# Layer 3 of a four-layer network: patch loads on GpSimd, a quarter's last turn finished ahead of the next matrices, nine of 24 matrix copies on ScalarE

## The chip, the cores and the metric

The kernel runs on one core of one Trainium2 chip. Its metric is the device time of one execution in microseconds (us). Beside the runs there is one profiled execution with its trace, and every stage and duration below is from that one.

## The reference, cut to what matters

A 16 x 64 x 64 x 256 tensor passes four layers, each `x = x + layer(groupnorm(x))`. The change lies in layer 3, an involution with a 7 x 7 window: every pixel makes its own 49 weights for each of 16 groups of 16 channels.

```python
r = relu((x @ w_reduce - mean) * (gamma / sqrt(var + eps)) + beta)     # 64 channels
kgen = (r @ w_span + b_span).reshape(B, H, W, 16, 49)                   # weights of each pixel
patches = 7 x 7 neighbours of x                                         # B, H, W, 49, 16, 16
out = einsum('bhwgk,bhwkgc->bhwgc', kgen, patches)
```

The layer's result is added to its input: that input is called the residual below.

## The kernel before, in words

The four layers run one after another, with some overlap; what each leaves for the next lies in HBM. Layer 2 is written in a hand-made order. Layer 3 is not: its instructions are put in order for each engine by a scheduler that works through the program's dependences, buffers and priorities, so a change of one buffer count or one queue moves other instructions too.

Layer 3 takes the image in tiles of 3 x 8 output pixels, whose inputs are 9 x 14 = 126 pixels: those fill the 126 rows of a TensorE operand. Layer 2 leaves in HBM, for each image i and each half h of the 256 channels, the array `strips`, out of which one tile row of eight tiles (`xw`, 128 rows of 4 KB, 512 KB) is loaded at once. There are 22 tile rows.

An image is worked in four quarters, (h, pr) = (0,0), (0,1), (1,0), (1,1): h is the half of the channels and pr which 64 channels of it. A quarter has two stages.

- `matrices(h, pr)`: for two pairs of groups, q = 0 and 1, twelve steps n each fill a PSUM tile `pk` (L1372, pool `wg`, three buffers) with four small products of the spread `span` of `w_span` and the reduced pixels `rt`, and a copy adds the bias `spanb` and puts it in the SBUF tile `wm`. The 24 copies of a quarter are split: where `n % 12 in (1, 3, 6, 8, 10)` ScalarE makes the copy in four instructions (L1382), else VectorE in one (L1387). `wm[q]` holds the banded weight matrices of all 176 tiles.
- eleven turns over `td`, each of two tile rows. `involution7` multiplies the patches by the matrices into PSUM `pa` (L1444; it uses the pool `wg` as well); ScalarE (L1453) and VectorE (L1454) mask and join the two groups' parts into `ex`. `finished` transposes `ex` into `po` (L1463), adds the residual that lies in `ot` (L1471) and returns the stores to the output. A turn is finished in the course of the next one, and its stores are issued (L1514) at the start of the one after.

Three things are fetched in the course of the turns, all by SyncE's queue, which issues in order and waits where an instruction waits:

- the residual of the next turn, `load_residual` (L1431), 96 KB in pieces of 256 bytes, into `ot` with three buffers. The output's store leaves from the same buffer, so a load has to wait for the store that empties it.
- in a quarter with pr = 1, after each turn, the two tile rows of the next half (L1420): the patches have 24 buffers for 22 tile rows, and both quarters of one half use the same ones.
- in the quarter (1,1) also a part of the next image's reduced pixels' input `c3` (L1320, 384 KB, two buffers), which `reduced` (L1339 `pr`, L1346) turns into `rt`. The next image's matrices need all of `rt`.

The loop of turns, whose order is the program's priority:

```python
for dst, src in store:
    nc.sync.dma_start(out=dst, in_=src)      # the stores of the turn before last
if td == 0:
    wm = matrices(h, pr)
ex = involution7(i, h, pr, td, wm, msk)
if pr == 1 and (i, h) != (NI - 1, 1):
    load_patches(...)
if last:
    store = finished(*last)                  # the turn before this one
if h == pr == 1 and i + 1 < NI:
    reduced(i + 1, td, cs.pop((i + 1, td)))
```

So the last turn of a quarter is finished after the next quarter's matrices and first turn were put into the program.

Of the kernel before, what the change touches and what calls it, by code (L numbers as in the profile page):

```python
# [9 lines left out]
F32 = mybir.dt.float32  # L10
# [5 lines left out]
P = 128  # L16
# [28 lines left out]
def network(ctx: ExitStack, tc: tile.TileContext, a: dict, out: bass.AP):  # L45
    nc = tc.nc
# [136 lines left out]
    with ExitStack() as st:  # L183
# [27 lines left out]
        wk = st.enter_context(tc.tile_pool(name="a_work", bufs=2))  # L211
# [428 lines left out]
    with ExitStack() as st:  # L640
        pc = st.enter_context(tc.tile_pool(name="s_const", bufs=1))
        wk = st.enter_context(tc.tile_pool(name="s_work", bufs=3))
# [22 lines left out]
        with tc.tile_pool(name="s_conv", bufs=1) as pcv:  # L665
# [4 lines left out]
                out=lsa.rearrange("p i j c -> p (i j c)"), in_=a["lsa_w"].partition_broadcast(P)  # L670
# [3 lines left out]
            for dj in range(7):  # L674
                dst = band if dj == 0 else term
# [52 lines left out]
        with tc.manual_schedule():  # L728
# [25 lines left out]
            for n, (ch, g) in enumerate(steps):  # L754
# [18 lines left out]
                b, k = g * 8, min(8, NI - g * 8)  # L773
# [8 lines left out]
        n = NI * NCH  # L782
# [100 lines left out]
    with ExitStack() as st:  # L883
        pc = st.enter_context(tc.tile_pool(name="b_const", bufs=1))
        wk = st.enter_context(tc.tile_pool(name="b_work", bufs=2))
# [403 lines left out]
    with ExitStack() as st:  # L1289
        pc = st.enter_context(tc.tile_pool(name="c_const", bufs=1))  # L1290
        wk = st.enter_context(tc.tile_pool(name="c_work", bufs=2))
# [5 lines left out]
        def cconst(name, shape, src=None):  # L1297
            t = pc.tile(shape, F32, tag=name, name=name)
            if src is not None:
                nc.sync.dma_start(out=t, in_=src)  # L1300
            return t

        wr3 = cconst("wr3", [P, 2, 64], a["w_reduce"].rearrange("(h p) f -> p h f", p=P))
        wr3t = cconst("wr3t", [P, 2, 2, 64])
        for k in range(2):
            nc.vector.tensor_copy(wr3t[:, :, k, :], wr3)
        span = cconst("span", [P, 16, SPAN], a["span"].rearrange("k (g s) -> k g s", g=16))
        spanb = cconst("spanb", [P, 16 * TILE_OUT], a["spanb"])
        gpar = cconst("gpar", [P, 2], a["gpar"])
# [45 lines left out]
        def matrices(h, pr):  # L1355


            wm = []
            for q in range(2):
                w = wm_p.tile([P, NTL, 2 * TILE_OUT], F32, tag="wm", name="wm")  # L1360
                wm.append(w)
                first = h * 8 + pr * 4 + q * 2
                for n in range(12):

                    pk = wg.tile([P, 2, CT], F32, tag="wg", name="pk")
                    pkv = pk[:, :, 0 : 2 * NTL].rearrange("p b (m t) -> p b m t", m=2)
                    for m in range(2):
                        for b in range(2):
                            gg, o = divmod(n * 4 + b * 2 + m, TILE_OUT)
                            s0 = SPAN - P - (o // TC * (TC + 6) + o % TC)  # L1370
                            half = slice(b * 64, b * 64 + 64)
                            nc.tensor.matmul(  # L1372
                                pkv[:, b, m],
                                lhsT=span[half, first + gg, s0 : s0 + P],
                                rhs=rto[half, o, :],
                                start=True, stop=True,
                            )
                    g0 = first * TILE_OUT + n * 4
                    dst = w[:, :, n * 4 : n * 4 + 4].rearrange("p t (b m) -> p b m t", b=2)
                    if n % 12 in (1, 3, 6, 8, 10):  # L1380
                        for m in range(4):
                            nc.scalar.activation(  # L1382
                                dst[:, m // 2, m % 2], pkv[:, m // 2, m % 2], AF.Identity,
                                bias=spanb[:, g0 + m : g0 + m + 1],
                            )
                    else:
                        nc.vector.tensor_tensor(  # L1387
                            dst, pkv,
                            spanb[:, g0 : g0 + 4].rearrange("p (b m) -> p b m", b=2).unsqueeze(
                                3  # L1390
                            ).broadcast_to([P, 2, 2, NTL]),
                            ALU.add,
                        )
            return wm
# [4 lines left out]
        def blocks(t, td):  # L1399

            if td * TR * HW + 4 * TB <= NT:
                return [t[0:TB]]
            return [t[0:TB, 0:2], t[0 : HW, 2]]

        def tokens(t, i, h, pr, td):

            t = t[i, :, h * P + pr * 64 : h * P + pr * 64 + 64]
            t0 = td * TR * HW
            if t0 + 4 * TB <= NT:
                return [t[t0 : t0 + 4 * TB].rearrange("(m p) c -> p m c", p=TB)]  # L1410
            return [
                t[t0 : t0 + 2 * TB].rearrange("(m p) c -> p m c", p=TB),
                t[t0 + 2 * TB : t0 + 2 * TB + HW],
            ]

        def load_patches(i, h, td):

            for ti in range(td, td + 2):
                xw = xw_p.tile([P, NTC, P], F32, tag="xw", name="xw")
                nc.sync.dma_start(  # L1420
                    out=xw.rearrange("p t c -> p (t c)"),
                    in_=strips[i, h].rearrange("r w t c -> (r w) (t c)")[
                        ti * TR * (TC + 6) : ti * TR * (TC + 6) + P
                    ],
                )
                xws[i, h, ti] = xw

        def load_residual(i, h, pr, td):
            ot = wk.tile([P, 4, 64], F32, tag="ot", name="ot", bufs=3)
            for dst, src in zip(blocks(ot, td), tokens(x3_d, i, h, pr, td)):  # L1430
                nc.sync.dma_start(out=dst, in_=src)  # L1431
            return ot
# [26 lines left out]
        def finished(i, h, pr, td, ex, ot):  # L1459

            po = sm.tile([P, 2, P], F32, tag="sm", name="po")
            for b in range(2):
                nc.tensor.transpose(po[0:TB, b, :], ex[:, b * TB : (b + 1) * TB], ident)  # L1463
            pov = po.rearrange("p b (k c) -> p k b c", k=2)
            otv = ot.rearrange("p (k b) c -> p k b c", k=2)
            if len(blocks(ot, td)) == 1:
                sides = [(slice(0, TB), slice(0, 2), slice(0, 2))]
            else:
                sides = [(slice(0, TB), 0, slice(0, 2)), (slice(0, HW), 1, 0)]
            for p, k, b in sides:  # L1470
                nc.vector.tensor_tensor(otv[p, k, b], pov[p, k, b], otv[p, k, b], ALU.add)  # L1471
            return list(zip(tokens(outs, i, h, pr, td), blocks(ot, td)))
# [3 lines left out]

        turns = [
            (i, h, pr, td)  # L1480
            for i in range(NI) for h in range(2) for pr in range(2) for td in range(0, NTR, 2)
# [4 lines left out]
        for td in range(0, NTR, 2):  # L1486
            load_patches(0, 0, td)
        res = [load_residual(*turns[0])]
        cs, last, store = {}, None, []
        for n, (i, h, pr, td) in enumerate(turns):  # L1490
            if h == pr == td == 0:

                pm = sm.tile([P, CT], F32, tag="sm", name="pm")
                for k in range(2):
                    for j in range(2):
                        nc.tensor.matmul(
                            pm[64 * k : 64 * k + 64, 2 * j : 2 * j + 2],
                            lhsT=ident[:, 64 * j : 64 * j + 64], rhs=rs3[:, i, :],
                            start=True, stop=True,
                        )  # L1500
                msk = small.tile([P, 2, 2, 2], F32, tag="msk", name="msk")
                nc.vector.tensor_tensor(
                    msk.rearrange("p j k g -> p (j k) g"),
                    pm[:, 0:4].unsqueeze(2).broadcast_to([P, 4, 2]),
                    gpar.unsqueeze(1).broadcast_to([P, 4, 2]),
                    ALU.mult,
                )
            if n + 1 < len(turns):
                res.append(load_residual(*turns[n + 1]))
                i1, h1, pr1, td1 = turns[n + 1]  # L1510
                if h1 == pr1 == 1 and i1 + 1 < NI:
                    cs[i1 + 1, td1] = load_reduced(td1, i1 + 1)
            for dst, src in store:
                nc.sync.dma_start(out=dst, in_=src)  # L1514
            if td == 0:
                wm = matrices(h, pr)
            ex = involution7(i, h, pr, td, wm, msk)
            if pr == 1 and (i, h) != (NI - 1, 1):
                load_patches(*((i, 1) if h == 0 else (i + 1, 0)), td)
            if last:  # L1520
                store = finished(*last)
            if h == pr == 1 and i + 1 < NI:
                reduced(i + 1, td, cs.pop((i + 1, td)))
            last = (i, h, pr, td, ex, res.pop(0))
# [110 lines left out]
```

## Time and profile before

| | |
|---|---|
| median of 3 runs | 10375.88 us (10372.54 to 10379.64) |
| profiled execution, its own time | 10364.39 us |
| its span, first to last instruction | 10362.3 us |
| mean granted clock of TensorE in it | 0.898 of full speed |
| TensorE matmul, weight load | 8062.1 us (78%), 5739.4 us (55%) |
| VectorE, ScalarE, GpSimd | 6725.2 us (65%), 5273.7 us (51%), 2347.8 us (23%) |
| layer 3, first pk matmul to the end | 6870 to 10362 us |
| DMA queue of SyncE | 1743.32 MB, 55.1% of the engines' span |

Engines: PE is TensorE's matmuls, PEld its weight loads, DVE VectorE, ACT ScalarE, POOL GpSimd, SP SyncE; a q marks an engine's queue of instructions, here mostly DMA issues. A row of a group gives the line, the engine, the tiles it writes and reads, their shapes and the count; then the total busy time and the mean in ns; then the engine's idle time just before such instructions and who ended most of it. A row of a table of stages gives for each stretch of time its length, the busy time and number of instructions of each engine, TensorE's granted clock, the mean busy share of the 16 DMA engines and the rate in GB/s. A row of the waits says who waited for whom: total us, times, the longest. A row of the timeline gives start, length, engine, line and tiles; neighbouring instructions of one kind are merged, so a length can hold waits between them.

### The profile page before, as it was taken

What the parts mean: (1) busy time and instruction counts of PE and PEld (TensorE: products, weight loads), DVE (VectorE), ACT (ScalarE), POOL (GpSimd) and SP (SyncE); (2) the same over time, 40 slices, a digit from 0 to 9 for tenths busy, and PEclk for the clock granted to TensorE, in tenths of its full rate; (3) what the DMA queues carried; (4) which work ended last, traced back from release to release, by engine and by line L of the source; (5) the groups of instructions that cost most, each with busy time, mean ns of one, the idle gap of its engine ahead of it and who ended that gap; (6) DMA issues with size and microseconds to landing.
All of it is one profiled execution on the core that took longest, in us unless ns stands there. A gap on an engine that the chain in (4) does not pass through costs nothing.

```text
span 10362.3 us, 216910 instructions
## 1 busy us (share of the span) xinstructions
PE 8062.1 (78%) x86488; PEld 5739.4 (55%) x86488; DVE 6725.2 (65%) x11456; ACT 5273.7 (51%) x12544; POOL 2347.8 (23%) x1193
## 2 busy tenths in 40 slices
PE   8888898888988675777778777727777777777777
PEld 5666666666666432554555555525555555555555
DVE  5666666666666555999999999924544545445454
ACT  4555555555555446666666665514444434444344
POOL 0111111111111002677777776710000000000000
PEclk9999999999999777989888888868998988988889
DMA  7433444334442247577777777665555555565554
GB/s 244 139 130 124 143 146 134 131 127 138 146 133 100 90 139 252 178 224 229 226 226 228 229 228 215 172 173 170 173 171 178 148 178 162 167 183 148 176 164 142
DMA packets 1648725, 1762.94 MB, mean 170 GB/s; under 512 B 641249, under 2 KB 1343026, under 8 KB 1646562
## 3 DMA queue, kind: packets, MB, share of 16 engines
q1 hardware_dynamic: 1635722, 1743.32, 55.1%
q8 instruction: 684, 11.21, 0.4%
q10 hardware_dynamic: 11992, 5.74, 0.3%
q14 instruction: 327, 2.68, 0.1%
HBM read 1234.54 MB, written 536.87 MB: 171 GB/s over the span
## 4 chain that ended last, share of the span: by engine, by line
PE 32%; DVE 27%; DMA 13%; issue 11%; ACT 11%; POOL 4%; SPq 2%; ACTq 0%; DVEq 0%; POOLq 0%
DVE pd L1106 7%; PE pa L1444 6%; DVE wm L1387 6%; PE pk L1372 5%; PE pq L297 5%; PE py L453 4%; DVE x L1274 3%; DMA c_d<-c 2%; ACT sq L462 2%; ACT wm L1382 2%; PE po L1463 2%; DMA out<-ot 2%; PE pr L1339 2%; DMA strips<-xc 2%; DVE y L458 1%
## 5 line engine op out<-in xcount | busy, mean ns | idle before, releaser
L297 PE MATMUL pq<-wq,xn 128*128 128x384 f32 x4096 | 1481.4, 501 | 61.3 <-DVE diag L346 20.9
L1372 PE MATMUL pk<-rt,span 64*128 64x176 f32 x12288 | 1260.7, 344 | 269.6 <-DVE wm L1387 150.2
L1106 DVE TENSOR_TENSOR pd<-xs,pw 128x576 f32<-128x576 f32 (+15 forms) x3072 | 1437.7, 545 | 8.7 <-PE pw L1060 5.2
L1387 DVE TENSOR_TENSOR wm<-pk,spanb 128x704 f32<-128x704 f32 x896 | 1155.9, 1342 | 352.9 <-PE pk L1372 280.9
L1372 PEld LDWEIGHTS pk<-rt,span 64*128 64x128 f32 x12288 | 1013.5, 200 | 502.9 <-DVE wm L1387 260.2
L1382 ACT ACTIVATE wm<-pk,spanb 128x176 f32<-128x176 f32 x2560 | 973.0, 543 | 575.7 <-PE pk L1372 494.9
L1117 POOL TENSOR_TENSOR pd<-pd 128x2048 f32<-128x2048 f32 (+2 forms) x384 | 1067.9, 2781 | 402.5 <-DVE pd L1106 382.4
L1444 PE MATMUL pa<-wm,xw 126*32 126x48 f32 x45056 | 764.1, 220 | 426.1 <-issue 359.8
L297 PEld LDWEIGHTS pq<-wq,xn 128*128 128x128 f32 x4096 | 754.6, 194 | 492.2 <-issue 46.3
L1454 DVE SCALAR_TENSOR_TENSOR ex<-pa,msk,ex 128x192 f32<-128x192 f32 x704 | 291.3, 414 | 1084.7 <-ACT ex L1453 1084.1
L1444 PEld LDWEIGHTS pa<-wm,xw 126*32 126x32 f32 x45056 | 633.7, 119 | 615.9 <-issue 498.4
L1453 ACT ACTIVATE ex<-pa,msk 128x192 f32<-128x192 f32 x704 | 296.4, 421 | 949.6 <-PE pa L1444 730.7
L1076 PE MATMUL pt<-ident,pad 128*128 128x128 f32 x4608 | 654.9, 298 | 148.2 <-ACT rt L1053 58.5
L1029 PE MATMUL px<-x2p,wis 128*128 128x512 f32 x1024 | 588.8, 725 | 197.5 <-ACT c L1131 165.7
L1076 PEld LDWEIGHTS pt<-ident,pad 128*128 128x128 f32 x4608 | 559.6, 154 | 304.7 <-ACT rt L1053 70.9
L1080 ACT COPY xs<-pt 128x512 f32<-128x512 f32 x1152 | 608.8, 587 | 189.3 <-PE pt L1076 188.7
L1274 DVE TENSOR_REDUCE x<-pd 128x512 f32<-128x4608 f32 x128 | 633.4, 4948 | 1.4
L453 PE MATMUL py<-wo,oT 128*128 128x256 f32 x2048 | 484.4, 388 | 55.2 <-DVE va L313 45.0
L1339 PE MATMUL pr<-c,wr 128*128 128x384 f32 (+1 forms) x704 | 337.4, 612 | 243.9 <-DMA c<-c_d 172.5
L1346 ACT ACTIVATE rt<-pr,b,sb 128x128 f32<-128x128 f32 x528 | 201.5, 451 | 616.6 <-PE pr L1339 554.3
L1471 DVE TENSOR_TENSOR ot<-po,ot 96x256 f32<-96x256 f32 (+2 forms) x768 | 286.7, 382 | 340.5 <-PE po L1463 187.5
L465 POOL TENSOR_TENSOR rsy<-ss,mhalf 128x4 f32<-128x4 f32 x128 | 129.8, 1014 | 1643.0 <-DVE ss L463 1643.0
(244 smaller groups left out, 13953.2 us busy)
## 6 DMA issues: line engine op xcount, KB each, us to landing
xw<-strips SPq DMA_DIRECT2D x704, 512.0 KB
xn<-x_d SPq DMA_DIRECT2D x256, 512.0 KB
x<-x_d SPq DMA_DIRECT2D x256, 512.0 KB
x_d<-x SPq DMA_DIRECT2D x256, 512.0 KB
strips<-xc SPq DMA_DIRECT2D x1464, 56.0 KB
xin<-in_x SPq DMA_DIRECT2D x256, 256.0 KB
x_d<-xc SPq DMA_DIRECT2D x128, 512.0 KB
xm<-x_d SPq DMA_DIRECT2D x128, 512.0 KB
```

The source lines that it names most:

```text
L297: nc.tensor.matmul(pq[:, dd, 0:384], lhsT=xn[:, h, tok], rhs=wq[:, h, hf * 384 : (hf + 1) * 384], start=(h == 0), stop=(h == 1),)
L453: nc.tensor.matmul(py[:, q, :], lhsT=oT[hf][:, q * P : (q + 1) * P], rhs=wo[:, hf, :], start=(hf == 0), stop=(hf == 1),)
L1029: nc.tensor.matmul(px, lhsT=w[:, h, fh * P : (fh + 1) * P], rhs=x2[:, h], start=(h == 0), stop=(h == 1),)
L1076: nc.tensor.transpose(pt[:, k, h * P : (h + 1) * P], lines[:, h, rc * 4 + e + k, 2 * j : 2 * j + P], ident,)
L1080: nc.scalar.copy(t[:, e : e + 2, 0:C], pt)
L1106: nc.vector.tensor_tensor(pd[:, :, o - oh * P : o - oh * P + n, :], xs[dj][:, di : di + 4, c0 : c0 + 9 * n].rearrange("p r (f k) -> p r f ...
L1117: nc.gpsimd.tensor_tensor(pd[..., 0:n], pd[..., 0:n], pd[..., n : 2 * n], ALU.add)
L1274: nc.vector.tensor_reduce(x3[:, :, P:C], pd1, AX.X, ALU.add)
L1372: nc.tensor.matmul(pkv[:, b, m], lhsT=span[half, first + gg, s0 : s0 + P], rhs=rto[half, o, :], start=True, stop=True,)
L1382: nc.scalar.activation(dst[:, m // 2, m % 2], pkv[:, m // 2, m % 2], AF.Identity, bias=spanb[:, g0 + m : g0 + m + 1],)
L1387: nc.vector.tensor_tensor(dst, pkv, spanb[:, g0 : g0 + 4].rearrange("p (b m) -> p b m", b=2).unsqueeze(3).broadcast_to([P, 2, 2, NTL]), AL ...
L1444: nc.tensor.matmul(pav[p0 : p0 + 32, :, tj * TC : (tj + 1) * TC], lhsT=xws[i, h, td + k][0:TILE_IN, tj, c0 : c0 + 32], rhs=wm[q][0:TILE_IN ...
```

## The change

GpSimd issues the patch loads. `ot` has four buffers. At the start of a quarter the last turn of the quarter before is finished and stored before `matrices` is called. Of the twelve copies of q = 0 ScalarE makes four (n = 1, 4, 6, 9), of q = 1 five as before. The layer's constant `wr3t` is loaded twice from HBM, in place of one load and two VectorE copies.

```diff
-        wr3 = cconst("wr3", [P, 2, 64], a["w_reduce"].rearrange("(h p) f -> p h f", p=P))
         wr3t = cconst("wr3t", [P, 2, 2, 64])
         for k in range(2):
-            nc.vector.tensor_copy(wr3t[:, :, k, :], wr3)
+            nc.sync.dma_start(
+                out=wr3t[:, :, k, :], in_=a["w_reduce"].rearrange("(h p) f -> p h f", p=P)
+            )
...
-                    if n % 12 in (1, 3, 6, 8, 10):
+                    if n in ((1, 4, 6, 9), (1, 3, 6, 8, 10))[q]:
                         for m in range(4):
                             nc.scalar.activation(
...
                 xw = xw_p.tile([P, NTC, P], F32, tag="xw", name="xw")
-                nc.sync.dma_start(
+                nc.gpsimd.dma_start(
                     out=xw.rearrange("p t c -> p (t c)"),
...
         def load_residual(i, h, pr, td):
-            ot = wk.tile([P, 4, 64], F32, tag="ot", name="ot", bufs=3)
+            ot = wk.tile([P, 4, 64], F32, tag="ot", name="ot", bufs=4)
...
             for dst, src in store:
                 nc.sync.dma_start(out=dst, in_=src)
+            store = []
             if td == 0:
+                if last:
+                    for dst, src in finished(*last):
+                        nc.sync.dma_start(out=dst, in_=src)
+                    last = None
                 wm = matrices(h, pr)
             ex = involution7(i, h, pr, td, wm, msk)
```

## The prediction

> **What bounds the kernel now.** I read the page's share of busy time first (TensorE 78%, VectorE 65%, ScalarE 51%, the DMA engines half busy in layer 3: nothing is full on average), then the costliest groups, then a table of stages for one image of layer 3, then the waits and SyncE's own timeline. Every part of the change lies in layer 3, which runs from 6870 us (first pk matmul) to 10362 us: 64 quarters, 54.6 us each. Its groups:
>
> ```profile
> L1372 PE MATMUL pk<-rt,span 64*128 64x176 f32 x12288 | 1260.7, 344 | 269.6 <-DVE wm L1387 150.2
> L1387 DVE TENSOR_TENSOR wm<-pk,spanb 128x704 f32<-128x704 f32 x896 | 1155.9, 1342 | 352.9 <-PE pk L1372 280.9
> L1382 ACT ACTIVATE wm<-pk,spanb 128x176 f32<-128x176 f32 x2560 | 973.0, 543 | 575.7 <-PE pk L1372 494.9
> L1444 PE MATMUL pa<-wm,xw 126*32 126x48 f32 x45056 | 764.1, 220 | 426.1 <-issue 359.8
> ```
>
> The stages of the image that starts at 8011.4 us, in pairs of matrices and turns for the quarters (h, pr) = (0,0), (0,1), (1,0), (1,1); the last row is what follows the last turn's pa:
>
> ```profile
> core 0: us, PE busy (x) PEld busy (x) DVE busy (x) ACT busy (x) POOL busy (x), PEclk, DMA share, GB/s
> 8011.40:8032.70 21.30, 18.82 (x193) 15.69 (x193) 16.67 (x13) 14.27 (x39) 0.00 (x0) 0.94 0.42 147
> 8032.70:8053.20 20.50, 14.20 (x723) 11.00 (x721) 8.01 (x21) 4.87 (x13) 0.00 (x0) 0.96 0.32 71
> 8053.20:8075.00 21.80, 19.55 (x200) 15.13 (x196) 17.97 (x18) 14.65 (x39) 0.00 (x0) 0.96 0.16 36
> 8075.20:8099.20 24.00, 14.12 (x717) 11.26 (x718) 6.56 (x16) 4.04 (x11) 0.00 (x0) 0.86 0.81 255
> 8100.90:8130.20 29.30, 24.80 (x196) 19.95 (x198) 18.66 (x20) 15.36 (x41) 0.00 (x0) 0.73 0.79 250
> 8130.40:8152.40 22.00, 15.71 (x726) 11.94 (x724) 8.33 (x20) 4.87 (x13) 0.00 (x0) 0.92 0.31 71
> 8152.40:8174.20 21.80, 19.94 (x195) 16.37 (x194) 17.82 (x17) 14.80 (x39) 0.00 (x0) 0.92 0.14 32
> 8174.40:8208.40 34.00, 24.38 (x745) 16.37 (x744) 7.09 (x18) 10.49 (x29) 0.00 (x0) 0.90 0.81 258
> 8208.40:8228.50 20.10, 12.01 (x61) 6.20 (x48) 3.39 (x10) 6.34 (x18) 0.00 (x0) 0.83 0.86 274
> ```
>
> The matrices keep TensorE busy (18.8 of 21.3 us); the turns do not, and they split in two kinds. With pr = 0 the DMA engines are a third busy and still the 11 turns take 20.5 to 22 us. With pr = 1, where patches are loaded, the DMA engines are 80% busy. The waits of this image, and SyncE's issues in its first turns, say why:
>
> ```profile
> SPq L1514 <- DVE ot L1471: 65.3, 22, 16.9
> SPq L1431 <- DMA out<-ot: 46.5, 30, 4.2
> DVE ot L1471 <- DMA ot<-x_d: 11.8, 8, 4.1
> PE pr L1339 <- DMA c<-c_d: 7.6, 3, 5.1
> ...
> 8036.51 0.31 SPq L1431 DMA_DIRECT2D ot<-x_d  x1
> 8036.99 3.80 SPq L1514 DMA_DIRECT2D out<-ot  x3
> 8040.88 2.67 SPq L1431 DMA_DIRECT2D ot<-x_d  x3
> 8045.06 2.05 SPq L1514 DMA_DIRECT2D out<-ot  x3
> 8047.16 1.74 SPq L1431 DMA_DIRECT2D ot<-x_d  x3
> ```
>
> SyncE issues three stores, then three loads, because ot has three buffers: a residual load waits for the store that empties its buffer, VectorE waits for the residual, and VectorE stands in order, so the next ex, the next pa bank and TensorE wait behind it. The bound of a turn is this ring of three buffers, not an engine.
>
> I also took the first and last pk and pa matmul of every quarter from the trace. Medians over the images, matrices / turns: (0,0) 21.3/21.0; (0,1) 21.2/24.2 and 1.5 to the next quarter; (1,0) 27.6/21.6; (1,1) 21.0/33.7 and a tail of 20.9.
>
> **What the Trainium skill says.** "DMA: Bandwidth & Descriptors", section "Anatomy of one DMA — SWDGE (gpsimd) path": a load issued by GpSimd costs about 2.0 us plus bytes/436e3, an estimate of 3.2 us for 512 KB, and many descriptors come out before their generation counts. No DMA of this trace is issued there. Same page, "Issuing engines are not separate DMA queues": all issuers share 16 DMA engines; only the issuer's time is saved. The 0.81 share at 255 GB/s agrees that patches are limited by the engines, not SyncE. Same page, "Queues, rings and completion order": each DMA engine goes round robin between queues, by packets; not shown here, with one busy data queue. "SBUF — State Buffer", "Who interferes with whom": VectorE instructions with at most one SBUF input and outside the two-port modes don't block GpSimd. The wm, ex and ot forms read one operand from PSUM; nothing here tests it.
>
> **The change, part by part.**
>
> *Four ot buffers.* A residual load issued at 8036.51 is waited for until 8040.02: 3.5 us. The store before it went out from 8034.30 and let that load go 2.2 us later. With 0.3 us of issue and 0.4 us of add the ring is 6.4 us long: 2.1 us a turn over three buffers (seen: 21.0/11 = 1.9, as the first are loaded ahead), 1.6 over four. TensorE's own pace is 1.32 us (pa at 8036.43, 8037.76, 8039.08). Four turns loaded ahead at 1.32 and seven at 1.6 make 16.5 us. (0,0) gains 4.5, (1,0) 5.1. Bounds: 14.5 (TensorE's pace) to no gain.
>
> *Patch loads on GpSimd.* 704 issues of some 0.47 us leave SyncE, and with them their waits for pa, which held residuals, stores and c3 loads behind them. On GpSimd's queue they come last, after layer 2's subtractions; nothing is queued behind them there, and only the pa that reads a patch waits for one. Their bytes stay: in this image 4096-byte packets fill 64 of 117 us of all DMA engines' time, 32 us for each 22 loads. In (0,1) residuals no longer queue behind two 512 KB loads, but the DMA engines get fuller, since loads now go as fast as pa frees buffers. I take the middle between 16.5 and today's 24.2: 20.5, a gain of 3.7. In (1,1) a turn also has pr (1.56 us) beside pa 0.89 and po 0.42: 2.9 us, 31.6 in all. c3 has two buffers and 384 KB loads, now beside the patches instead of behind them. I take 3.45 us a turn: 38 for turns and tail in place of 54.6, a gain of 16.6; bounds 32 and 54.6. All 22 patches need 32 us of DMA time, with c3 14 and residuals 9 at most 55, against 38 + 21 + 16 us until the last is used: not late. GpSimd's issue time per load is unknown: between nothing and the page's 3.2 us; I take 1 to 2 us, hidden as GpSimd is idle (0.00 in all rows).
>
> *Last turn ahead of the matrices.* Instruction order, before: in (1,0) three po pairs stand among the first 37 pk matmuls, and VectorE's ot additions stop wm copies where a residual is late; at a quarter's end SyncE stands up to 16.9 us at a store. After: one po pair after three pk matmuls, and additions after one copy. (1,0)'s matrices take 27.6 us, with 24.8 of TensorE's time in the image shown, at a clock of 0.73; I take 24.6, a gain of 3.0. The clock stays. The cost: po now waits at the head for the last ex (two instructions of 0.42 us), behind which pk waits: 0 to 0.8 us a quarter, I take 0.3, 20 us in all.
>
> *Nine of 24 copies on ScalarE.* VectorE gets one more copy (1.24 us when back to back: three in 3.73), 18.6 us of 21; ScalarE loses four instructions (1.54 us). pk has three banks in both, and their round trip sets the pace. I take 0. The range is -20 to +79 us (64 x 1.24, if VectorE became the bound of the stage).
>
> *wr3t loaded twice, no copies.* Two VectorE copies and a load go, two loads come, once, among layer 2's last stores: 0, within 3 us each way. The order at layer 3's start, with its single wait of 71 us for layer 2's stores, is the same.
>
> **Sum.** 4.5 + 3.7 + 8.1 + 16.6 = 32.9 us an image, 526 for 16. The last image's (1,1) loads nothing ahead and reduces nothing: 5 instead of 16.6, so 515. Off: 20 for po; and 60 for the clock, which is lowest where patches flow (0.73, 0.83) and will be asked for the same work in less time (3% of some 125 us of TensorE-paced work an image, an estimate). Net 435. The profiled execution had 10364.4 us (span 10362.3): 9929. The median of runs is 11.5 higher: **9940 us**.
>
> **Rivals.** *(a) Patches crowd out small transfers.* With up to eight patches in GpSimd's ring, residuals (256-byte packets) and c3 get a poor share; quarters with pr = 1 gain nothing, those with pr = 0 keep 4.5 + 8.1: 202 less 60: 10230. For it: the DMA share of 0.8 already. Against: today they stand behind the same loads in one queue. *(b) Better than forecast:* pr = 1 comes near TensorE's pace (17 and 33), 8.5 us more an image, 136: 9800; without the clock's loss 9740. *(c) Slower: GpSimd can't issue fast enough.* From the first pa of (0,1) to the last of (1,0) today lie 24.2 + 1.5 + 27.6 + 21.6 = 75 us for 22 loads, 3.4 us each; in the other half 97 us, 4.4 each. Beyond about 3.9 us of issue per load the kernel is slower. At 4.5: 24 us x 16 + 2 x 15 = 414: 10790. Against: the page's 3.2 us is mostly latency, which overlaps. *(d) Nothing:* what residuals gain, the clock takes: 10376.
>
> **How the numbers follow.** Forecast with (b): 0.66, (a) 0.19, (d) 0.03, (c) 0.12. A measurement of this kernel can tell about 0.2% from no change. Faster 0.85, same 0.03, slower 0.12. The range runs from 9690, (b) with a little more, to 10330, which takes in (a) and a copy stage slower by its bound.
>
> **What would show it.** Right: turns of pr = 0 at 15 to 17.5 us; SyncE alternating single loads and stores; no tail after the last pa of (1,1), and that quarter under 65 us; the matrices of (1,0) under 26; DMA bytes unchanged with a new queue. Wrong: TensorE waiting at pa for patches with the DMA share under 0.5 (c); ot additions waiting longer for their residuals in (0,1) than 4.1 us (a); wm copies of VectorE without idle time between them; a granted clock under 0.8 in most stages.

## The result, and the profile after

The kernel became **slower**: 10513.31 us in the median of four runs (10505.65 to 10523.07) against 10375.83 us before; the ratio is 1.0133 with a 95% interval of 1.0115 to 1.015. The profiled execution has a span of 10511.7 us, 149.4 more than before, and a mean granted clock of 0.889 (0.898). The forecast had been 9940.

First the costliest groups of layer 3 on the page of the kernel after (lines are one or two further down than before), and its DMA queues (packets, MB, share of 16 engines' span).

```profile
L1373 PE MATMUL pk<-rt,span 64*128 64x176 f32 x12288 | 1219.3, 335 | 244.1 <-DVE wm L1388 158.8
L1388 DVE TENSOR_TENSOR wm<-pk,spanb 128x704 f32<-128x704 f32 x960 | 1214.0, 1339 | 245.8 <-PE pk L1373 174.8
L1383 ACT ACTIVATE wm<-pk,spanb 128x176 f32<-128x176 f32 x2304 | 883.6, 539 | 655.3 <-PE pk L1373 580.8
...
L1421 POOL DMA_DIRECT2D xw<-strips x704 | 375.6, 538 | 3099.1 <-PE pa L1445 3025.5
...
L1445 PE MATMUL pa<-wm,xw 126*32 126x48 f32 x45056 | 784.4, 223 | 308.4 <-issue 261.1
```

```profile
q1 hardware_dynamic: 1534618, 1374.24, 44.2%
q0 software_dynamic: 101376, 369.14, 9.4%
q8 instruction: 684, 11.21, 0.4%
```

The 704 patch loads went to a queue of their own, q0, and cost GpSimd 538 ns each. q0 and q1 together carry 1743.38 MB, as SyncE's queue did alone (1743.32). VectorE has 960 copies of 1339 ns where it had 896, and stands idle before them for less time (245.8 us, 352.9 before). Nothing among these lines looks worse; the table of stages does. An image in the kernel after, in the order of the table shown in the prediction:

```profile
core 0: us, PE busy (x) PEld busy (x) DVE busy (x) ACT busy (x) POOL busy (x), PEclk, DMA share, GB/s
8077.50:8097.70 20.20, 17.98 (x194) 14.41 (x194) 18.00 (x16) 13.31 (x36) 0.00 (x0) 1.00 0.33 95
8097.60:8117.80 20.20, 15.27 (x726) 11.72 (x724) 8.45 (x20) 4.97 (x14) 0.00 (x0) 0.92 0.32 72
8118.00:8139.00 21.00, 18.70 (x196) 14.81 (x196) 18.51 (x18) 13.34 (x36) 0.00 (x0) 1.00 0.16 37
8139.00:8173.50 34.50, 17.90 (x724) 13.62 (x722) 7.96 (x19) 4.84 (x13) 10.68 (x20) 0.70 0.86 302
8174.30:8201.30 27.00, 21.19 (x196) 16.87 (x196) 18.93 (x19) 13.18 (x35) 0.46 (x1) 0.83 0.35 112
8201.30:8222.50 21.20, 15.23 (x725) 11.55 (x724) 8.55 (x20) 4.85 (x13) 0.00 (x0) 0.92 0.31 69
8222.70:8243.80 21.10, 18.77 (x196) 14.88 (x196) 18.52 (x18) 13.41 (x36) 0.00 (x0) 1.00 0.16 35
8243.80:8298.50 54.70, 34.87 (x769) 21.18 (x768) 8.58 (x21) 15.50 (x42) 10.66 (x20) 0.75 0.82 268
8298.50:8301.00 2.50, 2.15 (x18) 1.24 (x17) 1.39 (x5) 1.59 (x5) 1.06 (x2) 1.00 1.03 374
```

The fourth row, the turns of (0,1), took 24.0 us before and takes 34.5. In the next row, the matrices of (1,0), the DMA share fell from 0.79 to 0.35. Before, only a part of the patches was loaded in the turns of (0,1) (ten loads of 22 in the stage shown) and the rest flowed beside the matrices; now 20 are issued beside the turns. The medians over all images, taken from first and last pk and pa matmuls as before:

| quarter | matrices, before / after | turns, before / after | to the next, before / after |
|---|---|---|---|
| (0,0) | 21.3 / 19.9 | 21.0 / 20.9 | 0.1 / 0.5 |
| (0,1) | 21.2 / 20.8 | 24.2 / **34.3** | 1.5 / 0.7 |
| (1,0) | 27.6 / 26.2 | 21.6 / 21.1 | 0.1 / 0.5 |
| (1,1) | 21.0 / 20.8 | 33.8 / **53.3** | 21.0 / 2.7 |

The sums of the quarters changed by -0.4, +9.1, -1.8 and +2.2 us: 9.1 us an image, 146 for 16, of the 149 by which the spans differ. The loss lies in (0,1); the other three cancel. The tail of (1,1) did go, into its turns. And the turns with pr = 0 did not move.

The longest waits of SyncE's queue in this image (a store for the ex that its turn needs, a residual load for the store that empties its buffer), and then its timeline in the turns of (0,0):

```profile
SPq L1516 <- DVE ex L1455: 83.2, 23, 19.3
SPq L1432 <- DMA out<-ot: 57.2, 19, 9.7
```

```profile
8105.18 0.32 SPq L1516 DMA_DIRECT2D out<-ot  x1
8105.55 1.29 SPq L1432 DMA_DIRECT2D ot<-x_d  x1
8106.94 0.42 SPq L1516 DMA_DIRECT2D out<-ot  x1
8107.54 0.34 SPq L1432 DMA_DIRECT2D ot<-x_d  x1
```

SyncE now issues a store and a load in turn, as the prediction said it would when the ring of three buffers no longer binds; yet a turn takes as long as before. Of the 57.2 us that residual loads wait for stores, 0.2 lie in the turns of (0,0), where it had been 2.5, and 22.3 in those of (0,1). So that ring was not the bound of a calm turn. TensorE's timeline in the turns of the next (0,0) has what is:

```profile
8326.91 0.33 PE L1445 MATMUL pa<-wm,xw 126*32 126x48 f32 x10 [1.28 <-issue]
8327.17 0.42 PE L1464 MATMUL po<-ident,ex 128*96 128x128 f32 x2
8327.52 0.89 PE L1445 MATMUL pa<-wm,xw 126*32 126x48 f32 x64
8328.52 0.40 PE L1464 MATMUL po<-ident,ex 128*96 128x128 f32 x2
8328.85 0.74 PE L1445 MATMUL pa<-wm,xw 126*32 126x48 f32 x49
8330.74 0.37 PE L1445 MATMUL pa<-wm,xw 126*32 126x48 f32 x15 [1.16 <-issue]
```

In the midst of a bank, with its patches, its matrices and its bank there, TensorE stops for 1.2 us and waits for nothing that the profile names. Between the two stops stand 10 + 64 + 49 = 123 pa matmuls. That is a count of instructions, not of work: with as many weight loads and two po pairs, which have weight loads too, it makes 246 + 8 = 254. The kernel before has the same stops, in the turns of its (0,0); between these two stand 63 + 2 + 63 = 128 matmuls, 256 with their weight loads:

```profile
8040.04 0.89 PE L1444 MATMUL pa<-wm,xw 126*32 126x48 f32 x63 [0.73 <-issue]
8040.91 0.39 PE L1463 MATMUL po<-ident,ex 128*96 128x128 f32 x2
8041.23 0.88 PE L1444 MATMUL pa<-wm,xw 126*32 126x48 f32 x63
8043.56 0.23 PE L1444 MATMUL pa<-wm,xw 126*32 126x48 f32 x1 [1.45 <-issue]
```

The queue q8 ("instruction") moved 684 packets with 11.21 MB, 16 KB each. If they are TensorE's, its 172,976 matmuls and weight loads come to 64 bytes each, and a block is 256 instructions. The Trainium skill says the same ("Runtime: NRT & Kernel Launch", section "Instruction fetch mechanics": instructions are refilled in blocks of 16 KiB, 256 instructions, by a DMA queue that the sequencer drives); but it calls the cost of a block's boundary mostly hidden, and here the trace disagrees. Blocks start at 8324.10, 8328.15, 8332.10 and 8335.98, each takes about 1.3 us, and TensorE goes on 1.3 to 1.4 us after its end. One block each 3.9 us, and a turn is 132 instructions (64 pa, 2 po, as many weight loads): 11 turns are 1452 instructions or 5.7 blocks, at 3.9 us each 22.1 us. The 21 us of every calm quarter, before and after, is a little less; what was fetched ahead during the matrices can make the difference, which no run shows.

In the turns of (0,1) the same blocks come 6.5 us apart in the median (4.7 before), in (1,1) 9.7 us (6.0). That alone doesn't say that the fetch is what is late: TensorE, held up by anything else, uses up its blocks more slowly. And residuals are late there, as the timeline of all engines shows in the turns of the (0,1) that follows:

```profile
8380.77 0.55 PE L1445 MATMUL pa<-wm,xw 126*32 126x48 f32 x16
...
8383.75 0.72 PE L1445 MATMUL pa<-wm,xw 126*32 126x48 f32 x48 [2.43 <-issue]
...
8384.76 1.06 POOL L1421 DMA_DIRECT2D xw<-strips  x2 [3.16 <-PE pa L1445]
8388.27 0.42 DVE L1472 TENSOR_TENSOR ot<-po,ot 96x256 f32<-96x256 f32 x1 [8.68 <-DMA ot<-x_d]
8388.61 0.41 DVE L1455 SCALAR_TENSOR_TENSOR ex<-pa,msk,ex 128x192 f32<-128x192 f32 x1
```

A bank's pa stops after 16 matmuls and goes on 2.43 us later: the fetch. The addition shows the residual: VectorE stood for 8.68 us, and ex, next in its order, behind it. Over the whole kernel the wait of ot's additions for residuals grew from 137.6 to 316.3 us, its longest from 6.0 to 13.8. In (1,1) it is c3 that is late. The matmuls `pr`, which read it, before and after:

```profile
L1339 PE MATMUL pr<-c,wr 128*128 128x384 f32 (+1 forms) x704 | 337.4, 612 | 243.9 <-DMA c<-c_d 172.5
L1340 PE MATMUL pr<-c,wr 128*128 128x384 f32 (+1 forms) x704 | 334.6, 608 | 370.1 <-DMA c<-c_d 322.4
```

TensorE waits 150 us longer for c3, 10 us for each of the 15 images that have such loads.

So the **theory** for the experiments: patches on SyncE were held back by that queue's waits, and this left the DMA engines free for what is small and urgent: residuals, stores, c3 and TensorE's own instructions. On GpSimd nothing holds them back. The rivals: another part of the change is to blame; the residuals alone, or the fetch alone; the order within GpSimd's queue.

### The profile page after: what moved, and what is told of

The parts are those of the page before. It is cut to its first block, busy times and chain, and to the rows that moved or that the text cites. A ratio compares the mean times of both kernels' runs of the same rounds, so it can differ in the third digit from the quotient of the medians.

```text
span 10511.7 us, 217021 instructions
## 1 busy us (share of the span) xinstructions
PE 8057.6 (77%) x86488; PEld 5723.0 (54%) x86488; DVE 6797.4 (65%) x11518; ACT 5189.1 (49%) x12288; POOL 2723.6 (26%) x1897
## 3 DMA queue, kind: packets, MB, share of 16 engines
q8 instruction: 684, 11.21, 0.4%
## 4 chain that ended last, share of the span: by engine, by line
PE 29%; DVE 27%; DMA 19%; ACT 9%; issue 9%; POOL 4%; SPq 2%; ACTq 0%; DVEq 0%; POOLq 0%
DVE wm L1388 7%; DVE pd L1106 6%; PE pq L297 5%; DMA c<-c_d 4%; PE pk L1373 4%; PE pa L1445 4%; PE py L453 4%; DMA out<-ot 4%; DVE x L1274 3%; DMA c_d<-c 2%; ACT sq L462 2%; DMA ot<-x_d 2%; PE pr L1340 2%; PE po L1464 2%; DMA strips<-xc 2%
## 5 line engine op out<-in xcount | busy, mean ns | idle before, releaser
L1373 PE MATMUL pk<-rt,span 64*128 64x176 f32 x12288 | 1219.3, 335 | 244.1 <-DVE wm L1388 158.8
L1388 DVE TENSOR_TENSOR wm<-pk,spanb 128x704 f32<-128x704 f32 x960 | 1214.0, 1339 | 245.8 <-PE pk L1373 174.8
L1373 PEld LDWEIGHTS pk<-rt,span 64*128 64x128 f32 x12288 | 981.4, 194 | 474.5 <-DVE wm L1388 280.7
L1383 ACT ACTIVATE wm<-pk,spanb 128x176 f32<-128x176 f32 x2304 | 883.6, 539 | 655.3 <-PE pk L1373 580.8
L1421 POOL DMA_DIRECT2D xw<-strips x704 | 375.6, 538 | 3099.1 <-PE pa L1445 3025.5
L1445 PE MATMUL pa<-wm,xw 126*32 126x48 f32 x45056 | 784.4, 223 | 308.4 <-issue 261.1
L297 PEld LDWEIGHTS pq<-wq,xn 128*128 128x128 f32 x4096 | 752.2, 194 | 493.3 <-issue 46.7
L1340 PE MATMUL pr<-c,wr 128*128 128x384 f32 (+1 forms) x704 | 334.6, 608 | 370.1 <-DMA c<-c_d 322.4
```

What stands on the lines that cost most here:

```text
L297: nc.tensor.matmul(pq[:, dd, 0:384], lhsT=xn[:, h, tok], rhs=wq[:, h, hf * 384 : (hf + 1) * 384], start=(h == 0), stop=(h == 1),)
L1373: nc.tensor.matmul(pkv[:, b, m], lhsT=span[half, first + gg, s0 : s0 + P], rhs=rto[half, o, :], start=True, stop=True,)
L1383: nc.scalar.activation(dst[:, m // 2, m % 2], pkv[:, m // 2, m % 2], AF.Identity, bias=spanb[:, g0 + m : g0 + m + 1],)
L1388: nc.vector.tensor_tensor(dst, pkv, spanb[:, g0 : g0 + 4].rearrange("p (b m) -> p b m", b=2).unsqueeze(3).broadcast_to([P, 2, 2, NTL]), AL ...
L1445: nc.tensor.matmul(pav[p0 : p0 + 32, :, tj * TC : (tj + 1) * TC], lhsT=xws[i, h, td + k][0:TILE_IN, tj, c0 : c0 + 32], rhs=wm[q][0:TILE_IN ...
```

## The experiments

Stages are medians over images. A ratio is to the kernel before, run beside it on the same chip.

**1 and 2. Which part?** First the kernel after with `nc.sync.dma_start` for the patches; then the kernel before with `nc.gpsimd.dma_start` for them and nothing else.

```diff
 xw = xw_p.tile([P, NTC, P], F32, tag="xw", name="xw")
-nc.gpsimd.dma_start(
+nc.sync.dma_start(        # run 1, from after; run 2 is the reverse, from before
```

> The changed kernel with its patch loads back on SyncE; everything else of the change stays. Theory F (TensorE's instruction fetch sets the turns: one 16 KB block, 256 instructions, in 3.9 us when the DMA engines are calm, and in 6.5 us beside GpSimd's queue): the turns of (0,1) go back from 34.3 to about 24 us, turns and tail of (1,1) to about 54, turns with pr = 0 stay at 21; the small gains in the matrices stay: about 10300 us. Theory R (patches crowd out the residuals, and VectorE waits for those): the same way, and with four ot buffers (0,1) falls below 22: about 10230. Theory G (GpSimd issues too slowly): about 10200 or less.

> The kernel before with only its patch loads on GpSimd. Theory F: the turns of (0,1) rise from 24.2 to 34, those of (1,1) with tail from 54.7 to 56 or more: about 10550 us. Theory R: the three ot buffers make it worse than the whole change: 10650 or more. If the queue of the patches is not the cause: 10376.

Patches back on SyncE: 10351.35 us, 0.9982 (0.9975 to 0.999); turns of (0,1) 24.9 us, (1,1) 31.7 and a tail of 21.6. GpSimd's patches alone: 10541.22 us, 1.0161 (1.0144 to 1.0178); turns of (0,1) 33.4 us, (1,1) 52.2. The loss is that one line; with the patches on SyncE everything else in the change is worth 0.2% for the better.

**3. Four ot buffers alone**, from before, with the two loads of wr3t, without which there is no room for the buffer.

```diff
-ot = wk.tile([P, 4, 64], F32, tag="ot", name="ot", bufs=3)
+ot = wk.tile([P, 4, 64], F32, tag="ot", name="ot", bufs=4)
```

> The kernel before with four ot buffers only (wr3t is loaded twice, as in the change, since SBUF has no room otherwise). The prediction's ring of three buffers: turns with pr = 0 fall from 21 to 16.5 us: about 10220 us. Theory F: they stay at 21, and the total within 40 us of 10376.

10331.85 us, 0.996 (0.9944 to 0.9977). The turns of pr = 0 take 20.9 and 22.6 us, where 21.0 and 21.6 were. The ring of three buffers is refuted as their bound; the 0.4% comes from elsewhere, mostly (0,1)'s sum, 47.3 to 44.8.

**4. Half of the instructions.** The kernel after with half of the pa matmuls and weight loads, each matmul with twice the columns; the patches of every second tile are left out.

```diff
-for tj in range(NTC):
+for tj in range(0, NTC, 2):
...
-    pav[p0 : p0 + 32, :, tj * TC : (tj + 1) * TC],
+    pav[p0 : p0 + 32, :, tj * TC : (tj + 2) * TC],      # and rhs from two tiles of wm
```

> The changed kernel in which one pa matmul of 96 columns takes the place of two of 48: every second tile's patches are left out (its neighbour's are used), so TensorE streams the same columns with half the matmuls and weight loads. Queues, bytes and all else stay. Theory F: turns with pr = 0 fall from 21 to about 15 us or less, those of (0,1) from 34.3 to about 20, those of (1,1) from 53 to about 40: 9850 us. Theory R and theory G: the turns of (0,1) and (1,1) stay within 3 us of what they are, turns with pr = 0 stay at 21 (the ring): about 10500.

10303.63 us, 0.9938 (0.9923 to 0.9953). The turns of pr = 0 fall from 21 to 14.3 and 14.0 us, 1.3 a turn. From the table of stages of one image, the turns of (0,0) and of (0,1):

```profile
8043.00:8057.70 14.70, 13.39 (x374) 9.66 (x374) 7.79 (x18) 4.90 (x13) 0.00 (x0) 1.00 0.32 73
...
8080.20:8113.30 33.10, 15.80 (x374) 11.15 (x372) 7.89 (x18) 4.84 (x12) 10.69 (x20) 0.71 0.91 319
```

With the columns unchanged and the instructions halved a calm turn is a third shorter. Fewer instructions are also less work, but in the stages shown TensorE's busy time fell by 1.9 us only (15.27 to 13.39). The rest are the stops, and these are gone: over the whole kernel TensorE's idle time before pa went from 308.4 us, 261.1 of it "issue", to 47.9, of which 8.6 are "issue".

```profile
L1446 PE MATMUL pa<-wm,xw 126*32 126x96 f32 x22528 | 749.6, 259 | 47.9 <-DVE wm L1388 22.1
```

So the fetch was the bound of a calm turn. The turns of (0,1) remain at 32.9 us, and the waits of ot's additions for residuals grew to 404.3: there, fetch is not alone. The 20 us for (0,1) and the 9850 us of the fetch theory didn't come.

**5. No residual loads.** The kernel after without them (the output lacks the residual).

```diff
-for dst, src in zip(blocks(ot, td), tokens(x3_d, i, h, pr, td)):
-    nc.sync.dma_start(out=dst, in_=src)
...
-nc.vector.tensor_tensor(otv[p, k, b], pov[p, k, b], otv[p, k, b], ALU.add)
+nc.vector.tensor_copy(otv[p, k, b], pov[p, k, b])
```

> The changed kernel with the residual loads left out (VectorE copies po to ot in place of adding it; stores, patches, c3 loads and all queues stay). Theory R (in quarters with pr = 1 small loads are starved by GpSimd's patches): the turns of (0,1) fall from 34.3 us to 26 or less; those of (1,1) stay above 40, as c3 loads are starved too; turns with pr = 0 stay at 21: about 10370 us. Theory F alone (a fetch takes 6.5 us beside the patches): (0,1) stays above 31: about 10480.

10337.29 us, 0.9973 (0.9961 to 0.9985). The turns of (0,1) fall to 30.2 us only, with a block each 6.2 us: neither the 26 of the one theory nor the 31 of the other. The pa group's idle time put down to "issue" is 312.1 us in this run, 261.1 with residuals; the fetch has come to the fore. The matrices of (1,0) fall from 26.2 to 22.1: there, late residuals of the last turn had their share.

**6. Another queue.** The kernel after with the patches on ScalarE's queue.

```diff
-nc.gpsimd.dma_start(
+nc.scalar.dma_start(
```

> The changed kernel with the patch loads on ScalarE's queue. If it is any second queue full of patches that starves SyncE's small loads: the turns of (0,1) stay near 34 us and those of (1,1) near 53: about 10500 us. If it is the descriptors that GpSimd makes in software: both fall to the values of patches on SyncE or below (25 and 50): 10350 or less.

10659.6 us, 1.0284 (1.0268 to 1.0299), the slowest of all, with a time that neither theory had. The turns of (0,1) take 28.8 us, the matrices of (1,0) 33.9 and the tail of (1,1) 16.9: here patches flow partly beside the matrices again, while ScalarE has ex, copies and rt to make. I didn't separate what of it is the queue and what ScalarE's time; this run decides nothing.

**7. The same loads on GpSimd, but later.** All 22 loads of a quarter with pr = 1 wait for the ex of its last turn, by a GpSimd copy of one column into each buffer.

```diff
+if gate is not None:
+    nc.gpsimd.tensor_copy(xw[:, 0, 0:1], gate[:, 0:1])
 nc.gpsimd.dma_start(
...
-if pr == 1 and (i, h) != (NI - 1, 1):
-    load_patches(*((i, 1) if h == 0 else (i + 1, 0)), td)
+if pr == 1 and (i, h) != (NI - 1, 1) and td == NTR - 2:
+    for t in range(0, NTR, 2):
+        load_patches(*((i, 1) if h == 0 else (i + 1, 0)), t, ex)
```

> The changed kernel, in which the 22 patch loads of a quarter with pr = 1 start only when its last turn's ex is written (each buffer first gets one column of ex by GpSimd, so that the load has to wait), so they flow beside the next matrices, where no residual is waited for. Theories R and F together: turns of (0,1) near 21 us, (1,1) near 35 without a tail; the next matrices 22 to 28 at a lower clock, and the turns after them 21 to 25, since the last patches come then: about 195 us an image in place of 215: 10060 us. If patches are needed earlier than they then come, TensorE waits at pa for them in (1,0) and (0,0): 10400 or more.

**10038.55 us** (10035.76 to 10042.6), ratio 0.9685 (0.9671 to 0.9699), near the 10060 expected: 3.1% faster than before, 4.5% under the kernel after, and the fastest of all. Its image, from the matrices of (0,0) on:

```profile
7912.10:7932.40 20.30, 18.09 (x195) 14.47 (x194) 17.99 (x16) 13.43 (x36) 10.55 (x30) 1.00 0.95 352
7932.30:7959.40 27.10, 16.75 (x726) 12.68 (x724) 8.45 (x20) 4.93 (x13) 2.69 (x5) 0.87 0.74 255
7959.50:7980.70 21.20, 18.86 (x198) 14.93 (x196) 18.54 (x18) 13.49 (x36) 0.00 (x0) 1.00 0.14 30
7980.60:8001.60 21.00, 14.19 (x726) 10.74 (x724) 8.56 (x20) 4.89 (x13) 0.00 (x0) 1.00 0.32 73
8001.80:8022.90 21.10, 18.75 (x197) 14.87 (x196) 18.55 (x18) 13.40 (x36) 11.73 (x40) 1.00 0.87 316
8022.80:8050.00 27.20, 17.33 (x726) 13.01 (x724) 8.46 (x20) 4.97 (x14) 2.69 (x5) 0.81 0.75 261
8050.10:8071.20 21.10, 18.77 (x197) 14.85 (x195) 18.53 (x18) 13.42 (x36) 0.00 (x0) 1.00 0.15 33
8071.20:8103.70 32.50, 28.24 (x769) 17.36 (x768) 8.58 (x21) 15.23 (x42) 0.00 (x0) 1.00 0.59 155
```

The first and fifth rows carry the patches at 352 and 316 GB/s and yet take 20 to 21 us: matrices, with 1.5 blocks of instructions and no residuals, don't mind. Turns of (0,1) are at 20.8 us, those of (1,1) at 31.1. The rest of the patches costs the turns of pr = 0 some 6 us (26.8 and 26.4, medians). Same bytes, same queue, another time: what hurts is the company of the turns. In (1,1) the waits for c3 went with it: 63.6 us in the whole kernel, where there were 322.4.

**8. From the eighth turn on.** The same edit with another time: eight turns' loads wait for the eighth turn's ex, and the last three turns' loads for their own.

```diff
-if pr == 1 and (i, h) != (NI - 1, 1) and td == NTR - 2:
-    for t in range(0, NTR, 2):
+if pr == 1 and (i, h) != (NI - 1, 1):
+    for t in range(0, 16, 2) if td == 14 else [td] * (td > 14):
```

> As the kernel whose patch loads wait for the last turn, but the first 16 loads wait only for the eighth turn's ex, the others for their own turns' ex. The patches begin some 6 us earlier. If what counts is the sum of patches beside turns, nothing is gained: turns of (0,1) and (1,1) grow by 5 us, those after the matrices shrink from 26.6 to 21.5: 10040 us, within 40. If a turn suffers less at the start of the stream than at its end: 9980.

10191.51 us, 0.9822 (0.9806 to 0.9838): slower than run 7 by 153 us, where I had expected it at or below it. The turns of pr = 0 are calm (21.8 and 21.9), but the tail of (1,1) grew to 9.0 us and the matrices after pr = 1 to 27.0 and 26.5. The tail is seen at its end, in the timeline:

```profile
8149.52 0.52 SPq L1321 DMA_DIRECT2D c<-c_d  x1
...
8155.93 2.05 PE L1340 MATMUL pr<-c,wr 128*128 128x256 f32 x4 [5.27 <-DMA c<-c_d]
```

The last c3 load went out beside patches, and 6.4 us passed from its issue to the `pr` that reads it; rt needs it, and all pk of the next image need rt. Why the matrices became longer, though in run 7 more patches flow beside them, isn't settled.

**9. Smaller packets.** The kernel after with each patch load split in two, of rows of 2 KB.

```diff
-nc.gpsimd.dma_start(
-    out=xw.rearrange("p t c -> p (t c)"),
+for s in range(2):
+    nc.gpsimd.dma_start(
+        out=xw[:, 4 * s : 4 * s + 4].rearrange("p t c -> p (t c)"),
...
```

> The changed kernel with each patch load split in two loads on GpSimd, of rows of 2 KB in place of 4 KB; same bytes. If the DMA engines take turns between queues descriptor by descriptor, a small transfer waits half as long each time: the turns of (0,1) fall from 34.3 to below 29 us, the interval between instruction fetches there from 6.5 to about 5.2: about 10400 us. If they take turns by larger portions, or by queue depth: unchanged, 10513, or up to 60 us slower by twice the issues.

10469.34 us, 1.009 (1.0075 to 1.0105); turns of (0,1) 31.8 us, a block each 6.3. The Trainium skill says that each DMA engine takes its queues in turn, a packet at a time ("DMA: Bandwidth & Descriptors", section "Queues, rings and completion order"). Its packet holds several descriptors, though, typically 9 to 17; if one of the patches has as many rows as before, rows of half the length would halve what a small transfer waits for. No run shows how many it has. The turns of (0,1) lost 2.5 us of the 10 that had come, and 1.5 of these came back as a longer wait before the next matrices (0.7 to 2.2 us). The direction agrees, the size is a quarter at most. The length of a patch row isn't the main thing.

**10. The late loads on SyncE.** Run 7 with `nc.sync.dma_start`; the one-column copy stays with GpSimd.

```diff
-nc.gpsimd.dma_start(      # run 7
+nc.sync.dma_start(
```

> As the kernel whose patch loads wait for the last turn, but issued by SyncE. If the time at which patches flow is all that counts: 10040 us, within 40. If GpSimd's own queue is needed, because the next residuals and stores stand behind 22 loads on SyncE: the turns after the matrices grow from 26.6 to above 30: 10150 or more, and still faster than the kernel before.

10065.12 us, 0.9702 (0.9685 to 0.9719). The two intervals overlap: no difference between the queues is shown, and it is below 0.5%; when the loads flow is worth 3%.

**11. Both chains gone.** Edits 4 and 5 together: half of the instructions, no residual loads; the output lacks both, as there.

> The kernel after with both edits at once: half of the pa matmuls and weight loads (the patches of every second tile are left out), and no residual loads (the output lacks the residual). Theory: in (0,1) the late residuals and TensorE's instruction fetch are two chains of nearly equal length, and taking away one uncovers the other (34.3 us became 32.9 without half the instructions, 30.2 without residuals). With both gone the turns of (0,1) fall to 15 to 20 us; (1,1) keeps a bound of its own, the late c3 loads, about 46 us. Calm turns 14, so some 14 us an image less than with half the instructions alone: about 10080. Rival: a third thing bounds (0,1), the patch flow itself, 22 loads at 1.35 us each: the turns stay at 28 to 31 us, and the time is about 10230.

10111.83 us, 0.9737 (0.9721 to 0.9753), near the theory's time; but the turns of (0,1) take 27.7 us, against its 15 to 20 and just under the rival's 28. A new wait of VectorE, for the stores that free `ot` (from the waits of this kernel), and the rate of the DMA engines in one such stage, in fortieths of its 27.4 us, show what holds them now:

```profile
DVE ot L1473 <- DMA out<-ot: 340.8, 110, 5.4
```

```profile
GB/s 0 0 0 0 24 42 173 353 407 359 371 377 371 409 403 420 389 389 404 407 410 408 409 407 410 406 405 412 404 414 403 413 404 407 403 388 403 409 408 408
```

Once the loads flow, the engines run at some 405 GB/s without a pause. 22 loads of 0.524 MB at that rate are 28.5 us, about as long as the turns. This is the third thing that the rival named; what ties the turns to it is the wait for stores. That they couldn't be shorter beside the same loads isn't shown. The calm turns are at 14.0 us as in run 4. The matrices of (1,0) are at 26.2 again, now without residuals, so what run 5 gained there isn't the residuals' alone; what else it is stays open. (1,1) has 46.7 and a tail of 5.6, against 53.3 and 2.7: residuals and fetch are only a small part of that quarter. The waits for c3 are likely to be the larger one (292.9 us in run 5, and 63.6 in run 7, whose (1,1) is fast); a kernel without the c3 loads wasn't tried.

The turns of (0,1) in four kernels make one table:

| us | with residuals | without |
|---|---|---|
| all pa instructions | 34.3 | 30.2 |
| half of them | 32.9 | 27.7 |

The two together bring 6.6 us, little more than the 4.1 and 1.4 that they bring alone; most of what separates 34.3 from a calm 21 stays. The traces show what takes the place of what. This table has TensorE's stops of over 0.4 us in the turns of (0,1), in us an image: those in the midst of a bank, and those before a po, which end when VectorE has made an ex or an addition to ot. VectorE makes both in order, and the addition waits for a residual or for the store that empties its buffer.

| kernel | in a bank | before po |
|---|---|---|
| before | 7.1 | 0.3 |
| after | 5.6 | 9.1 |
| run 4, half of the instructions | 0.5 | 15.5 |
| run 5, no residuals | 9.8 | 0.2 |
| run 11, both | 0.4 | 9.8 |

So of the 10 us that the change added to (0,1) nearly 9 are VectorE's late additions, not the fetch. Without residuals the fetch takes up a good part of the time, without the fetch the residuals do, and without both the stores.

## Why the prediction was wrong, step by step

By quarters, (0,0), (0,1), (1,0), (1,1), the forecast had gains of 4.5, 3.7, 8.1 and 16.6 us an image; 0.4, -9.1, 1.8 and -2.2 came. Two steps failed: the ring as the bound of a turn, and patches on GpSimd as a gain in the quarters with pr = 1.

- **"The bound of a turn is this ring of three buffers, not an engine"**, and with it 4.5 + 5.1 us: wrong. The stages moved by 0.1 and 0.5 (run 3: 0.1, and 1.0 the wrong way). TensorE's instruction fetch was the bound; run 4 showed it. The sign was in the fence that I had shown: the pa group was idle for 426.1 us, 359.8 of it "issue". I read the wait for a residual at 8040.02 as the cause of that turn's length, while the trace of before has a pa matmul at 8040.04 after 0.73 us of "issue", one instruction into its bank. And of the 46.5 us that I had shown of residual loads waiting for stores only 5.4 lie in the turns with pr = 0. The 1.32 us as TensorE's pace between the stops fits run 4's 1.3 a turn, which has half as many, wider matmuls and so doesn't measure it.
- **"The middle between 16.5 and today's 24.2: 20.5" for (0,1)**: this is the step that made the sign wrong. It measured 34.3, 10.1 worse instead of 3.7 better, by late residuals and the additions and ex behind them (9.1 us of stops before po, where there were 0.3). I had the number that warns against 20.5 in the next lines: 22 loads take 32 us of DMA time. I used it for (1,1) as a question of being late, and didn't put it beside the turns of (0,1), where the loads would now flow at once. I had also bounded the stage by today's 24.2 at the worst, as if a wait in a queue could only cost; it was the throttle that left the engines room for small transfers. "The DMA engines get fuller" was said and priced at nothing. I had also taken the share of 0.81 at 255 GB/s for engines that limit the patches; the same stage moved 302 GB/s after the change and some 405 in run 11, so they had room left.
- **(1,1), 54.6 to 38**: turns and tail became 56.0, in size the largest miss. The tail went, as said (2.7 us left), but the turns took it up: TensorE now waits for c3 there, 10 us an image more in all. Run 7, without patches there, has 31.1 for the turns: 2.9 us a turn and 31.6 were about right for a quarter without patches. The 3.45 us a turn that I took for the company of patches measured 53.3 / 11 = 4.85.
- **Last turn ahead, 3.0 us from the matrices of (1,0)**: 1.4 came, and the credit isn't clear. With the patches on SyncE (run 1) the stage has 27.8 us, no gain; against run 2 (29.1) the changed kernel gains 2.9. po's wait of 0.3 us a quarter measured 0.4 where it shows (0.1 to 0.5 us to the next quarter).
- **Nine of 24 copies at 0, wr3t at 0**: within their bounds, as far as can be seen; VectorE's 64 further copies cost nothing visible, and (0,0)'s matrices even fell by 1.4, of which run 2, without the new copies, has 1.0.
- **The clock, 60 us for denser work**: wrong in its reason. The mean did fall (0.898 to 0.889), but in a kernel that got slower. It was lowest where TensorE stops for long: in the table after it is 0.70 in the row with TensorE busy for 52% of the time and 1.00 in the matrices of (0,0) and (0,1) with 89%; 0.68 is the median of the turns of (0,1) (0.82 before). The two fastest orders of loads on GpSimd, runs 7 and 8, have means of 0.916 and 0.92. The busy share of a stage doesn't settle its clock, though: the turns of (0,1) in run 7 have 1.00 with 68%, the matrices of (1,0) before 0.73 with 85%, just after turns with longer stops. The Trainium skill has it so ("TensorE: Matmul & The Clock Gate", section "Part 1: The HAM clock gate": the default is throttled, activity releases it), and in the main these numbers agree.
- **The rivals.** (a), patches crowd out small transfers, had the right mechanism: its mark, ot additions that wait longer than 4.1 us in (0,1), is there (13.7 in the image shown). Its price was wrong: I let pr = 1 "gain nothing" where it lost, and left pr = 0 its gain. (c), the one rival on the slow side, is refuted: an issue costs 0.54 us, not 3.9. My slow case had the wrong mechanism, and 0.12 was too little, as a crowding that costs more than it brings was in no case.

## What to carry to other kernels

An in-order queue's waits can be a throttle that something urgent lives on. Before loads are set free, multiply them by the time each takes of full DMA engines and hold that beside the stage in which they will flow; if it is longer, try another stage (here the matrices) rather than another queue. Idle time put down to "issue", at equal counts of short instructions, was the instruction fetch here, and fewer, wider instructions took it away.

## What of the hardware was not expected

- TensorE's instruction blocks of 16 KB, one each 3.9 us, leave a stop of 1.2 us per 256 instructions where these are pairs of weight load and 48-column matmul. Beside patches and without residuals (run 5) the stop is 2.1 us in the median. The queue that brings them has 0.4% of the engines' span.
- GpSimd issues a 512 KB load in 538 ns, and the load lands 7.5 us later (median) beside others.
- A residual of 96 KB in 256-byte pieces kept its addition waiting for up to 13.8 us in the kernel after, 6.0 in the one before, where SyncE's waits throttled the patches.
- In one stage the DMA engines were busy for 0.81 of the time at 255 GB/s (with residuals and stores in 256-byte pieces), in another for 0.95 at 352 GB/s (run 7, patches beside the matrices): the share alone doesn't tell how much room is left.
